# A graph layer and an attention layer on one core: own orders for the opening and the last group, and one pair of exponentials moved behind two copies

## The chip, the core and the metric

The kernel runs on one core of one Trainium2 chip. The metric is the device time of one execution in microseconds, taken as the median of several runs. A profiled execution adds a trace of every instruction on the engines: PE (TensorE matmuls; PEld is its weight loads), DVE (VectorE), ACT (ScalarE), POOL (GpSimd) and SP (SyncE, which here only issues DMAs).

## What is computed

There are 64 inputs of 256 nodes with 512 features, and one 256 x 256 adjacency matrix of ones and zeros. Layer 0 is a graph layer, layer 1 is attention with 8 heads of 64 over the same graph; each has a residual and a layernorm.

```python
def _L0_gnn_ref(x, adj, W, b):
    Wi, Wj = (W[:, :Din], W[:, Din:])
    mi = jnp.einsum('bkd,od->bko', x, Wi)
    mj = jnp.einsum('bkd,od->bko', x, Wj)
    deg = a.sum(axis=1)
    return deg[None, :, None] * (mi + b) + jnp.einsum('ij,bjo->bio', a, mj)
...
x = _layernorm(x + _L0_gnn_ref(x, adj, L0_gnn_W, L0_gnn_b), axis=-1)
# q, k, v = x @ W.T + b, split in heads; scores = q k / 8, -inf where adj == 0; softmax; @ v
x = _layernorm(x + _L1_gnn_ref(x, adj, Wq, bq, Wk, bk, Wv, bv, Wo, bo), axis=-1)
```

## The kernel before, in words

**Groups.** Two inputs are a group; there are 32 groups. The loop over g runs attention of group g and, in between, layer 0 of group g + 1, so that TensorE always has matmuls that do not wait for a softmax. Line numbers in this section are those of the kernel before; lines of the form L281 in the profile are those of the helper `matmul`, so groups of instructions are told apart by their tiles.

**Layer 0** of one input b (`l0_inputs`, L461, `l0_steps`, L483): x is split in a rounded part xhi and a rest xlo (`split_x`, L340, on ACT and POOL; POOL also adds the bias times degree, degb, to x). For each of four chunks of 128 features, four matmuls multiply xhi and xlo with `graph`, which holds diag(deg) and the transposed adjacency side by side, into a bank pa. ACT copies three quarters of it to xl (L475), and DVE makes the four sums xS from xl and pa (L478 to L481). Then seven steps, each four matmuls of 128 x 256, form the product with the weights by the seven-product scheme of Strassen and Winograd: the right-hand factors are the blocks of w0 and four combinations T1 to T4 of them, the left-hand ones xl and xS. DVE adds each result to xh (L497); steps 6 and 7 end in a layernorm (`norm`: statistics on DVE, the power -0.5 on POOL, shift and apply on ACT). `h_transpose` brings the result into hT, with features on partitions.

**Layer 1.** `qk_steps`, `v_steps` and `o_steps` use the same seven-product scheme for both inputs of a group at once: 28 matmuls of 128 x 256 each. Their factors (the weights' blocks and T1 to T4, made once by `make_factors` and kept in DRAM) are streamed in by `bring`, eight ahead. Attention goes in four slots, of two pairs of heads each: `scores` (L709), then on DVE the mask is added (L717), ACT takes the exponential (L721), POOL sums the two halves to pk (L724); `values` (L742) multiplies by v into pav, `divide` (L781) makes the denominators den, their reciprocal rden, spreads them with eight small DMAs and lets POOL multiply. The last slot of a group divides at once on DVE (L771, L772). `fold_value_bias` (L402) puts the value bias through wo into the output bias once.

**What sets the order.** The kernel is written in a tile framework which puts instructions on each engine's queue, and adds waits. Instructions under `in_order`, all matmuls among them, keep the program's order; the others the framework may move. Each engine works through its own queue in order. Banks of PSUM come from three pools: two double banks for scores (`score_banks`), one for pav, and three for everything else (`bank`), so that a product which takes a bank waits until the last reader of the bank's former tile is done.

**Around the change.** In the opening (L288 to L362) the DMAs are issued as: adjacency, x of input 0, the bias b_bc, four quarters of the layer 0 weights, x of input 1. DVE builds aT from the transposed adjacency, from that the tile `exact`, degb, and then `graph` as a rounded copy of exact; T1 to T4 of w0, a check that the rounding lost nothing (`inexact`), and maskT follow. Layer 0 of input 0 runs chunk by chunk, xhi and xlo in turn. Then come make_factors of wq, the fold, and the rest of group 0's layer 0, with the other make_factors between (L832 to L856). In slot u of a group the list `work[u]` of layer 0 items is run after the first of the slot's two exponentials; in the third slot the first item is `l0_inputs` of the group's second input, second half. The last group has no next layer 0: its slots stand alone, and then `o_steps` and `finish_steps` run as in every group.

Of the kernel before, what the change touches and what calls it, by code (L numbers as in the profile page):

```python
# [225 lines left out]
def unshifted_path(ctx, tc, flag, x, adj, wiT, wjT, b0, wqT, bq, wkT, bk, wvT, bv, woT, bo, out):  # L226
# [71 lines left out]
    nc.sync.dma_start(out=b_bc, in_=b0.to_broadcast([P, D]))  # L298
    w0 = const.tile([P, 7, NC, H], F32, name="w0")

    for n, w, j in ((B11, wiT, 0), (T3, wiT, 1), (B22, wjT, 1), (B21, wjT, 0)):
        nc.sync.dma_start(out=w0[:, n], in_=w.rearrange("(c p) o -> p c o", p=P)[:, :, j * H:(j + 1) * H])
    load_x(1)
# [21 lines left out]
    transposed_graph(nc, a, aT, ident, ps_m, "mm")  # L325
    deg = small.tile([P, NT], F32, tag="deg", name="deg")
    nc.vector.tensor_reduce(deg, a, AX.X, ALU.add)
    exact = p1.tile([P, NT, 3 * P], F32, tag="oS", name="exact")
    inexact = const.tile([P, 1], F32, name="inexact")
    for t in range(NT):  # L330
        nc.vector.tensor_copy(exact[:, t, (1 - t) * P:(3 - t) * P], aT[:, t, :])
        nc.vector.tensor_scalar(exact[:, t, 2 * t * P:(2 * t + 1) * P], ident, deg[:, t:t + 1], None, ALU.mult)
    for t in range(NT):
        nc.vector.tensor_scalar(degb[:, t, :], b_bc, deg[:, t:t + 1], None, ALU.mult)

    nc.vector.tensor_copy(graph, exact)
# [3 lines left out]
    def split_x(b):  # L340

        if b < B:
            xhi[b] = p1.tile([P, NT, D], F32R, tag="xhi", name="xhi")
            in_order(nc.scalar.copy(xhi[b], xh[b]))
            xlo[b] = p1.tile([P, NT, D], F32R, tag="xlo", name="xlo")
            in_order(nc.gpsimd.tensor_tensor(xlo[b], xh[b], xhi[b].bitcast(F32), ALU.subtract))
            in_order(nc.gpsimd.tensor_tensor(xh[b], xh[b], degb, ALU.add))

    split_x(0)

    def combine_right(f):

        in_order(nc.vector.tensor_sub(f(T1), f(T3), f(B11)))
        nc.vector.tensor_sub(f(T2), f(B22), f(T1))
        nc.vector.tensor_sub(f(T4), f(B21), f(T2))
        nc.vector.tensor_sub(f(T3), f(B22), f(T3))

    combine_right(lambda n: w0[:, n])
    nc.vector.tensor_tensor(exact, exact, graph.bitcast(F32), ALU.not_equal)
    nc.vector.tensor_reduce(inexact, exact.rearrange("p t n -> p (t n)"), AX.X, ALU.max)  # L360

    nc.vector.tensor_scalar(maskT, aT, 0.0, MASK, ALU.is_equal, ALU.mult)  # L362


    def load_bias(b, name):
        t = const.tile([P, NC], F32, tag=name, name=name)
        nc.sync.dma_start(out=t, in_=b)
        d = const.tile([P, 2], F32, tag=name + "d", name=name + "d")
        nc.vector.tensor_sub(d, t[:, 2:4], t[:, 0:2])
        return t, d  # L370

    bq_sb, bqd = load_bias(bq, "bq")
    bk_sb, bkd = load_bias(bk, "bk")
    bv_t = small.tile([P, NC], F32, tag="bvt", name="bv_t")
# [27 lines left out]
    def fold_value_bias(raw):  # L402

        pb = bank("pb")
        spread = p3.tile([P, NC, P], F32, tag="pk", name="spread")
        nc.vector.tensor_copy(spread, bv_t.unsqueeze(2).to_broadcast([P, NC, P]))
        for c in range(NC):
            h, kc = divmod(c, 2)
            nc.tensor.matmul(pb, spread[:, c], raw[:, h, kc].rearrange("p j o -> p (j o)"),
                             start=(c == 0), stop=(c == NC - 1))  # L410
        nc.vector.tensor_add(bo_bc, pb, bo_bc)
# [48 lines left out]

    def l0_inputs(b, half, borrow=False):  # L461


        if half == 0:
            xl[b] = p2.tile([P, NC, 3, P], F32, tag="xl", name="xl")
            a11, a12, a22 = (xl[b][:, :, m, :] for m in range(3))
            xS[b] = left_blocks(a11, a12, None, a22, p2.tile([P, 4, NC, P], F32, tag="xS", name="xS"))
        for c in (2 * half, 2 * half + 1):
            cs = slice(c * P, (c + 1) * P)
            pa = score_banks("pa")[:, 0, :] if borrow else bank("pa")  # L470
            parts = [(t, part) for t in range(NT) for part in (xhi[b], xlo[b])]
            for n, (t, part) in enumerate(parts):
                matmul(pa[:, t * P:(t + 3) * P], part[:, t, cs], graph[:, t, :],
                                 start=(n == 0), stop=(n == len(parts) - 1), skip_group_check=True)
            nc.scalar.copy(xl[b][:, c].rearrange("p m n -> p (m n)"), pa[:, :3 * P])  # L475
            _, a12, a22, a21 = (pa[:, m * P:(m + 1) * P] for m in range(4))
            f = xS[b]
            nc.vector.tensor_add(f["S1"][:, c], a21, f["A22"][:, c])  # L478
            nc.vector.tensor_sub(f["S3"][:, c], f["A11"][:, c], a21)
            nc.vector.tensor_sub(f["S2"][:, c], a22, f["S3"][:, c])  # L480
            nc.vector.tensor_sub(f["S4"][:, c], a12, f["S2"][:, c])  # L481
# [227 lines left out]
    def scores(g, u):  # L709


        made = []

        def exponentials(w, ps):
            i, pr = divmod(w, NC)
# [9 lines left out]
            made.append((pe, pk))  # L725

        later = []
        for w in (2 * u, 2 * u + 1):
            i, pr = divmod(w, NC)
            n0 = i * N  # L730
            ps = score_banks("ps").rearrange("p j (t q) -> p j t q", t=NT)
            for kc in range(NT):
                for j in range(2):
                    rows = slice(j * DH, (j + 1) * DH)
                    matmul(ps[:, j, kc, :], kT[g][rows, pr, n0 + kc * P:n0 + (kc + 1) * P],
                           qT[g][rows, pr, n0:n0 + N], start=True, stop=True)
            later.append(lambda w=w, ps=ps: exponentials(w, ps))
        return made, later

    products = []  # L740

    def values(g, u, made):  # L742
        i, half = divmod(u, NC // 2)
        n0 = i * N
        if u == 0:
            aoT[g] = p1.tile([P, NC, NB * N], F32, tag="aoT", name="aoT")
            oS[g] = pair_blocks(aoT[g], "oS")
        pav = ps_v.tile([P, 2, N], F32, tag="av", name="pav")
        for pp, (pe, _) in enumerate(made):
            for kc in range(NT):  # L750
                for j in range(2):
                    h0 = (2 * (2 * half + pp) + j) * DH
                    matmul(pav[j * DH:(j + 1) * DH, pp, :], vv[g][:, i, kc, h0:h0 + DH], pe[:, j, kc, :],
                           start=(kc == 0), stop=(kc == NT - 1))
# [3 lines left out]
        dst = aoT[g][:, 2 * half:2 * half + 2, n0:n0 + N]  # L758
        if u < SLOTS - 1:
            nc.scalar.copy(dst, pav)  # L760
            divide(dst, [pk for _, pk in made])
            return

        den = bank("den").rearrange("p (r q) -> p r q", r=2)
        for pp, (_, pk) in enumerate(made):
# [3 lines left out]
        for pp in range(2):  # L769
            rden = p2.tile([P, N], F32, tag="rden", name="rden")  # L770
            in_order(nc.vector.reciprocal(rden, den[:, pp, :]))  # L771
            in_order(nc.vector.tensor_mul(dst[:, pp, :], pav[:, pp, :], rden))  # L772
            inverses.append(rden)
        return inverses

    def end_values(g, inverses):
        combine_left(oS[g], in_order)
# [50 lines left out]
    for g in range(-1, NG):  # L828
        for name in (["wo"] if g >= 0 else []) + (["wq", "wk", "wv"] if g + 1 < NG else []):
            queue.extend((name, n) for n in (RIGHT_O if name == "wo" else RIGHT))  # L830

    load_x(2)  # L832
    raw_o, raw_q, raw_k, raw_v = (load_raw(w, t) for w, t in ((woT, "aoT"), (wqT, "kT"), (wkT, "v"), (wvT, "qT")))
    head = layer0(0)
    run(head[0])
    run(head[1])
    make_factors(wqT, "wq", raw_q)
    fold_value_bias(raw_o)
    run(head[2])
    make_factors(wkT, "wk", raw_k)  # L840
    run(head[3])
    make_factors(wvT, "wv", raw_v)
    run(head[4][:2])
    make_factors(woT, "wo", raw_o)
    for _ in range(AHEAD):
        bring()
    run(head[4][2:])
    q = qk_steps(0, qT, "qT", bq_sb, bqd)
    run(q[:1] + head[5] + head[6] + q[1:])
    run(with_output_bias(0, qk_steps(0, kT, "kT", bk_sb, bkd)))  # L850
# [5 lines left out]
    waiting, later = scores(0, 0)  # L856
    run(later + v[5:])
    for g in range(NG):
        more = g + 1 < NG
        load_x(NB * (g + 2))  # L860
        load_x(NB * (g + 2) + 1)
        work = layer0(g + 1) if more else [[] for _ in range(SLOTS + 3)]
        run(work[0])
        for u in range(1, SLOTS):
            values(g, u - 1, waiting)
            waiting, later = scores(g, u)
            run(later[:1] + work[u][:1] + later[1:] + work[u][1:])
        inverses = values(g, SLOTS - 1, waiting)
# [3 lines left out]
        end_values(g, inverses)  # L872
        run(rest[2:] + o[2:5] + work[SLOTS + 1] + o[5:6] + work[SLOTS + 2] + o[6:])
        end = finish_steps(g)
        if more:
            q = qk_steps(g + 1, qT, "qT", bq_sb, bqd)
            k = with_output_bias(g + 1, qk_steps(g + 1, kT, "kT", bk_sb, bkd))
            v = v_steps(g + 1)
            run(q[:5] + end[:1] + q[5:6] + end[1:2] + q[6:7] + end[2:3] + k[:1] + end[3:4] + k[1:] + end[4:] + v[:1])
            split_x(NB * (g + 2))  # L880
            run(v[1:5])
            waiting, later = scores(g + 1, 0)
            run(later + v[5:])
        else:
            run(end)
# [51 lines left out]
```

## Time and profile before

| what | us |
|---|---|
| median of 3 runs | 3264.04 (3263.74 to 3264.42) |
| the profiled execution, its own time | 3264.57 |
| its span in the trace | 3262.8 |
| mean granted TensorE clock | 0.997 of full speed |
| TensorE busy with matmuls | 3197.6 (98% of the span) |
| DVE, POOL, ACT busy | 1894.1, 1507.8, 1109.6 |
| DMA | 341.69 MB, mean 105 GB/s |

The profile's page gives busy time by engine, then the span in 40 slices of 81.6 us with a digit for the busy tenths of each. A line of a timeline gives start, duration, engine, line, operation, what it writes and reads (buffer numbers left out), and in brackets how long the engine was idle before it and what ended that. A line of the waits view gives who waited for whom, the sum, how many times and the longest. A stage line gives length, busy time of PE, PEld, DVE, ACT and POOL with the number of instructions, the granted clock, and what the DMA engines did. One matmul of the program in full float32 shows as two in the trace, 0.216 us apart for 256 columns at the full clock; the 384-column matmuls of the graph stage are in a rounded format and 0.18 us apart.

### The profile page before, as it was taken

The page shows a single profiled execution, that of the slowest core. Times are in us where ns is not written, and L with a number is a line of the kernel's source. Part 1 is how long each engine was busy: PE and PEld are TensorE (multiplying, and loading weights), DVE is VectorE, ACT ScalarE, POOL GpSimd, SP SyncE. Part 2 cuts the span into 40 slices and gives each one's busy share as a digit, 9 for nine tenths or more (in the row PEclk, how much of TensorE's full clock was granted, in tenths as well). Part 3 has the DMA queues.
Part 4 walks back from the last instruction along what each step waited for, and adds up shares of the span by engine and source line. Part 5 has one row for each costly group of instructions (what it writes and reads, how often), then busy time and mean ns, then how long its engine had stood idle before and what let it go on. Part 6 is the DMA issues. An engine that isn't in the chain of part 4 may idle for free. (4 is left out here: it accounts for less than half of the span.)

```text
span 3262.8 us, 48286 instructions
## 1 busy us (share of the span) xinstructions
PE 3197.6 (98%) x17422; PEld 2620.6 (80%) x17422; DVE 1894.1 (58%) x3852; ACT 1109.6 (34%) x2145; POOL 1507.8 (46%) x1193
## 2 busy tenths in 40 slices
PE   7999999999999999999999999999999999999997
PEld 6788887788887888878888778888788887888875
DVE  5655556555565555665555655556555566555564
ACT  2333333333333333333333334333333333333332
POOL 2454344544445444445434454444544444544443
PEclk9999999999999999999999999999999999999998
DMA  7234432344323344223333234432234432344322
GB/s 239 66 107 123 120 102 67 100 118 122 114 69 90 114 120 122 86 75 107 120 120 107 66 97 119 121 116 72 87 110 122 121 90 74 104 119 122 97 66 80
DMA packets 258000, 341.69 MB, mean 105 GB/s; under 512 B 29920, under 2 KB 155104, under 8 KB 257760
## 3 DMA queue, kind: packets, MB, share of 16 engines
q1 hardware_dynamic: 257760, 338.55, 34.8%
q8 instruction: 143, 2.34, 0.3%
q14 instruction: 97, 0.79, 0.1%
HBM read 275.52 MB, written 37.75 MB: 96 GB/s over the span
## 5 line engine op out<-in xcount | busy, mean ns | idle before, releaser
L439 POOL TENSOR_TENSOR rstd<-ve,mhalf 128x1 f32<-128x1 f32 x256 | 140.4, 549 | 822.3 <-DVE below L437 821.7
L281 PE MATMUL po<-w,xS 128*128 128x256 f32 x2048 | 474.3, 382 | 3.8
L281 PE MATMUL st<-hS,factor 128*128 128x256 f32 x2048 | 452.5, 379 | 0.0
L724 POOL TENSOR_TENSOR pk<-pe 128x512 f32<-128x512 f32 x256 | 323.2, 1273 | 269.3 <-ACT pe L721 269.3
L281 PEld LDWEIGHTS po<-w,xS 128*128 128x128 f32 x2048 | 383.9, 190 | 76.6 <-DVE xh L497 16.2
L281 PEld LDWEIGHTS st<-hS,factor 128*128 128x128 f32 x2048 | 389.1, 190 | 52.9
L281 PE MATMUL po<-w,xl 128*128 128x256 f32 x1536 | 366.7, 385 | 23.8 <-ACT xl L475 13.8
L721 ACT ACTIVATE pe<-pe 128x1024 f32<-128x1024 f32 x256 | 271.1, 1059 | 342.6 <-DVE pe L717 342.6
L281 PEld LDWEIGHTS po<-w,xl 128*128 128x128 f32 x1536 | 280.0, 190 | 91.2 <-ACT xl L475 26.2
L281 PE MATMUL st<-hT,factor 128*128 128x256 f32 x1536 | 343.9, 380 | 0.7 <-ACT hT L545 0.7
L603 DVE TENSOR_TENSOR u<-st,u 128x512 f32<-128x512 f32 x96 | 66.4, 692 | 476.3 <-PE st L281 464.2
L717 DVE TENSOR_TENSOR pe<-ps,maskT 128x1024 f32<-128x1024 f32 x256 | 296.9, 1201 | 65.3 <-PE ps L281 65.3
L497 DVE TENSOR_TENSOR xh<-po,xh 128x256 f32<-128x256 f32 (+1 forms) x384 | 173.4, 459 | 267.9 <-POOL xh L505 176.8
L281 PEld LDWEIGHTS st<-hT,factor 128*128 128x128 f32 x1536 | 292.9, 191 | 41.0 <-ACT hT L545 0.9
L281 PE MATMUL pav<-pe,v_sb 128*64 128x256 f32 x2048 | 251.8, 388 | 6.2 <-ACT pe L721 6.1
L281 PE MATMUL ps<-qT,kT 64*128 64x256 f32 x2048 | 256.3, 390 | 0.0
L281 PEld LDWEIGHTS ps<-qT,kT 64*128 64x128 f32 x2048 | 187.7, 187 | 67.7 <-issue 50.5
L281 PE MATMUL st<-factor,oS 128*128 128x256 f32 x1024 | 238.3, 381 | 2.2 <-issue 2.2
L281 PE MATMUL st<-factor,hS 128*128 128x256 f32 x1024 | 234.8, 382 | 0.0
L792 DVE RECIPROCAL rden<-den 128x256 f32<-128x256 f32 x96 | 168.8, 1758 | 97.1 <-PE den L281 93.4
L444 ACT ACTIVATE shift<-below,rstd 128x1 f32<-128x1 f32 x256 | 75.3, 294 | 427.0 <-POOL rstd L439 407.8
L281 PEld LDWEIGHTS st<-factor,hS 128*128 128x128 f32 x1024 | 191.9, 190 | 35.4 <-issue 10.6
(110 smaller groups left out, 5031.4 us busy)
## 6 DMA issues: line engine op xcount, KB each, us to landing
xh<-in_x_dram SPq DMA_DIRECT2D x64, 512.0 KB, 4.1
factor<-wq SPq DMA_DIRECT2D x128, 256.0 KB, 2.7
factor<-wk SPq DMA_DIRECT2D x128, 256.0 KB, 2.6
factor<-wv SPq DMA_DIRECT2D x128, 256.0 KB, 4.2
factor<-wo SPq DMA_DIRECT2D x128, 256.0 KB, 2.7
out_dram<-xh SPq DMA_DIRECT2D x64, 512.0 KB, 3.8
factor<-in_wqT_dram SPq DMA_DIRECT2D x96, 256.0 KB, 2.7
factor<-in_wkT_dram SPq DMA_DIRECT2D x96, 256.0 KB, 2.7
```

What stands on the lines that cost most here:

```text
L281: in_order(nc.tensor.matmul(*args, **kw))
L439: nc.gpsimd.tensor_tensor(rstd, ve, mhalf, ALU.pow)
L444: order(nc.scalar.activation(shift, below, AF.Identity, scale=rstd))
L497: nc.vector.tensor_add(dst, src, dst)
L603: nc.vector.tensor_add(new("u2"), bank["y"], k["u1"])
L717: nc.vector.tensor_add(pe.rearrange("p j t q -> p j (t q)"), ps.rearrange("p j t q -> p j (t q)"), maskT.rearrange("p t q -> p (t q)").uns ...
L721: in_order(nc.scalar.activation(flat, flat, AF.Exp, scale=QSCALE, accum_out=etot[:, NB * g + i, pr:pr + 1]))
L724: nc.gpsimd.tensor_tensor(pk, pe[:, :, 0, :], pe[:, :, 1, :], ALU.add)
L792: nc.vector.reciprocal(rden, den)
```

## The change

Three parts.

**The opening.** b_bc is loaded after the first quarter of w0. `graph` is written directly: two diagonals by DVE, then two copies out of the transposes' banks, with ACT copying the same banks to aT. degb, the bias differences and the check of `inexact` become functions that are called later. Input 0 is multiplied with all its xhi first, then all xlo (`first_inputs`), two of its banks borrowed from the scores' pool; step 3 of layer 0 comes ahead of step 2. The raw weights are loaded in the order wq, wk, wv, wo instead of wo, wq, wk, wv. make_factors and the fold go to other places: wq between the steps of input 0, wk before the steps of input 1, the fold after the first query product, wv and wo inside the query and key products, whose steps 2 and 3 change places for the query.

```diff
-    transposed_graph(nc, a, aT, ident, ps_m, "mm")
...
+    for t in range(NT):
+        nc.vector.tensor_scalar(graph[:, t, diagonal(t)], ident, deg[:, t:t + 1], None, ALU.mult)
+    for t in range(NT):
+        pt = bank("pt_a")[:, :N]
+        for i in range(NT):
+            transpose(pt[:, i * P:(i + 1) * P], a[:, i, t * P:(t + 1) * P], ident)
+
+        nc.vector.tensor_copy(graph[:, t, edges(t)], pt)
+        nc.scalar.copy(aT[:, t, :], pt)
...
+    def first_inputs(b):
+
+        input_tiles(b)
+        pas = [score_banks("pa")[:, 0, :] if c < 2 else bank("pa") for c in range(NC)]
+        for k, part in enumerate((xhi[b], xlo[b])):
+            for c in range(NC):
+                for t in range(NT):
+                    graph_product(b, c, pas[c], k * NT + t, t, part)
+                if k == 1:
+                    take_input(b, c, pas[c])
...
+    first_inputs(0)
+    in_order(nc.vector.tensor_sub(w0s[T3], w0s[B22], w0s[T3]))
+    p, q = l0_steps(0), l0_steps(1)
+    run([p[0], p[2], p[1]])
+    split_x(1)
+    run(p[3:5])
+    bias_steps()
     make_factors(wqT, "wq", raw_q)
-    fold_value_bias(raw_o)
-    run(head[2])
+    run(p[5:])
+    l0_inputs(1, 0, True)
+    l0_inputs(1, 1)
     make_factors(wkT, "wk", raw_k)
...
     q = qk_steps(0, qT, "qT", bq_sb, bqd)
-    run(q[:1] + head[5] + head[6] + q[1:])
-    run(with_output_bias(0, qk_steps(0, kT, "kT", bk_sb, bkd)))
+    run(q[:1])
+    fold_value_bias(raw_o)
+    h_transpose(1, 1, True)
+    h_transpose(1, 0, True)
+    run([q[2], q[1], *q[3:5]])
+    make_factors(wvT, "wv", raw_v)
+    run(q[5:])
+    k = with_output_bias(0, qk_steps(0, kT, "kT", bk_sb, bkd))
+    run(k[:4])
+    make_factors(woT, "wo", raw_o)
+    run(k[4:])
```

**The third slot.** `scores` and `values` now work on one pair of heads, and the loop calls them in twos in the same order as before. The one difference in groups 0 to 30: in the third slot both exponentials (mask, exponential, sum) stand after the first item of `work`, that is after the graph products of the second half and the copies of them; before, the first exponential stood ahead of it.

```diff
+            later = [scores(g, w), scores(g, w + 1)]
+            part = work[w // 2]
+            n = 0 if w == NB * NC - 2 else 1
+            run(later[:n] + part[:1] + later[n:] + part[1:])
```

**The last group** has code of its own. It goes pair by pair, with the scores two pairs ahead, and its output projection is plain: 16 matmuls of 128 x 512 with wo, which is loaded whole (1 MB) into the place of hT, instead of 28 of 128 x 256 and the sums. The first quarter of the projection stands ahead of the last pair's values, and each quarter is followed by its own addition, layernorm and store of 256 KB.

```diff
+    for w in range(last + 1):
+        values(g, w)
+        multiply()
+        if w == last - 1:
+            project(0, 0, (0, 1, 2, 3))
+            finish(0, 0)
+        elif w % 2 and w < last:
+            divide_two(g, w)
+        if w + 2 <= last:
+            scores(g, w + 2)()
+    inverses = divide_at_once(g, last)
+    project(0, 1, (0, 1, 2, 3))
+    finish(0, 1)
+    project(1, 0, (0, 1))
+    project(1, 1, (0, 1))
+    end_values(inverses)
+    for t in range(NT):
+        project(1, t, (2, 3))
+        finish(1, t)
```

## The prediction

> **What bounds the kernel now.** I read the page's busy shares first, then its slices, then busy time by stage, then TensorE's waits, then the timeline of one group.
>
> ```profile
> PE 3197.6 (98%) x17422; PEld 2620.6 (80%) x17422; DVE 1894.1 (58%) x3852; ACT 1109.6 (34%) x2145; POOL 1507.8 (46%) x1193
> ...
> PE   7999999999999999999999999999999999999997
> ```
>
> TensorE is the bound, and only the first and the last of the 40 slices (81.6 us each) are not full. The stages, cut at the first graph product (13.14), the first key product (73.68), the first value product (102.89), the last group's first scores (3201.68) and its first output product (3233.56):
>
> ```profile
> 0.00:13.14 13.14, 1.09 (x4) 0.75 (x5) 6.09 (x13) 2.33 (x2) 5.92 (x11) 1.00 0.78 257
> 13.14:73.68 60.54, 51.97 (x225) 43.45 (x225) 39.44 (x93) 13.88 (x29) 11.22 (x9) 0.97 0.71 245
> 73.68:102.89 29.21, 29.21 (x145) 25.32 (x143) 10.40 (x20) 8.94 (x17) 14.93 (x9) 1.00 0.52 143
> 102.89:3201.68 3098.79, 3074.97 (x16818) 2523.76 (x16817) 1804.45 (x3678) 1068.23 (x2068) 1451.01 (x1142) 1.00 0.35 102
> 3201.68:3233.56 31.88, 25.67 (x177) 15.33 (x176) 16.82 (x15) 11.46 (x20) 15.96 (x15) 0.89 0.14 39
> 3233.56:3262.80 29.24, 14.66 (x60) 11.95 (x58) 16.88 (x35) 4.79 (x9) 8.80 (x9) 0.83 0.11 39
> ```
>
> Length first, then TensorE's busy time, then the other engines; the third number from the end is the granted clock. TensorE idles 12 us before 13.14, 8.6 us up to 73.68, 24 us in the whole loop, 21 us after 3201.68. There is nothing else to win but work itself. The loop's 24 us are two waits per group:
>
> ```profile
> PE po L281 <- ACT xl L475: 13.8, 31, 0.8
> PE po L281 <- DVE xS L481: 10.0, 33, 2.6
> PE pa L281 <- DVE graph L336: 7.9, 1, 7.9
> PE pav L281 <- ACT pe L721: 6.1, 3, 2.2
> ```
>
> 31 waits of 0.445 us for the graph stage's copy xl, and (10.0 - 3.7 in the opening) / 31 = 0.20 us for xS. The third slot of one group:
>
> ```profile
> 1932.13 0.56 ACT L760 COPY aoT<-pav 128x512 f32<-128x512 f32 x1
> 1935.62 1.06 ACT L721 ACTIVATE pe<-pe 128x1024 f32<-128x1024 f32 x1 [2.92 <-DVE pe L717]
> 1936.58 0.19 ACT L721 ACTIVATION_READ_ACCUMULATOR pe<-pe 128x1 f32 x1
> 1936.67 0.84 ACT L475 COPY xl<-pa 128x384 f32<-128x384 f32 x2
> ...
> 1935.72 1.03 PE L281 MATMUL po<-w,xl 128*128 128x256 f32 x4
> 1937.18 1.13 PE L281 MATMUL po<-w,xl 128*128 128x256 f32 x4 [0.43 <-ACT xl L475]
> 1938.52 1.97 PE L281 MATMUL po<-w,xl 128*128 128x256 f32 x8 [0.20 <-DVE xS L481]
> ```
>
> ACT's copies stand behind the first exponential, though their graph product was complete at 1935.2.
>
> **The change: the loop.** Set side by side, the two programs differ in groups 0 to 30 in one thing: ACT's two xl copies now stand ahead of the first exponential. The order on PE, DVE, POOL and SP and what each waits for are the same. The first copy can start at 1935.2 (the fourth pa matmul starts at 1934.85 and takes 0.34), the second at 1935.95, both done by 1936.4; the matmul that waited till 1937.18 was due at 1936.60. That wait goes. What is late next is the x bank's successor: step 2 takes a bank whose last reader is an xS subtraction on DVE, and DVE adds two masks first (L717, 1934.42, 2.29 us), till 1936.7. Then xS begins at 1936.7 instead of 1937.16, and step 2 starts 1.36 us behind that as now (1938.52 - 1937.16): 1938.06. **0.45 us a group, times 31: 14 us.** Bounds: nothing, if DVE holds step 2 where it is; and the whole start-to-start excess of both places, (1937.18 - 1936.60) + (1938.52 - 1938.04) = 1.06 us, 33 us. I take 14, since the DVE rows set it. What is queued behind: both exponentials end at about 1938.6 as now (the second waited for DVE until 1937.4 anyway, they follow each other in 1.1 us); the first pk sum on POOL comes 0.8 us later, the second 0.1, and the denominators that need them stand at 1944.79. So the exponentials' delay is hidden under the 4 us of step products and transposes.
>
> **The opening.** Now DVE waits for b_bc until 8.16 (degb), then makes exact, aT, maskT and graph, and the first pa starts at 13.14. After: a 3.61 to 4.04, deg to 4.76, two diagonals (0.47 for both) to 5.25, two copies out of the transposes' banks straight to graph (0.37 each, the aT row) to 6.0; ACT copies aT behind them (0.37 each) to 6.5, then xhi (1.04): pa at 7.6, **5.5 us sooner**. Here the row is 6.0 for the graph, and ACT's aT copies wait for DVE's in the built program.
>
> [...]
>
> From there by hand: 16 pa matmuls (twelve at 0.32, as in the rows after 13.14, then 0.18) to 12.3; step 1 to 14.0. The last quarter of w0 lands at 14.0 as before, T4 needs it (1.21) to 15.25, then 16 xS operations start 0.20 apart; the 14th frees step 2's bank at 18.2. So the wait for xS stays (1.9 us, was 2.6). Step 2 and four more, 1.73 each, to 26.9; the second graph's pa (2.9, now without its 1.7 wait) to 29.75; its step 1 waits 1.15 for the last xl copy, which stands on ACT behind two layernorm operations; seven steps and two transposes to 44.1. Query product 1 to 45.85. The value-bias fold (8 x 0.43) now stands where TensorE waited for the second graph's layernorm (2.5 + 0.7 us, and a half-rate stretch to 64.7); it waits 0.75 for its spread behind that layernorm's DVE chain, ends at 50.05; transposes 0.85, six products 10.4: 61.35. Then a new wait: DVE does the last qT addition (0.88 for two) and only then the u3 one, and the key's first product takes the bank that they free: 1.15. **Key products start at 62.5 instead of 73.68: 11 us.** Bounds: 5.5, if all later waits come back as they are; 5.5 + 8.6 + 1.7 (the half-rate stretch) = 15.8.
>
> **The last group.** Now each slot waits through scores, two mask additions, two exponentials (7.4 to 7.9 us a slot), then come output products 1, two reciprocals (1.76 each), the S sums, 7 products, four layernorms in a row, two 512 KB stores. After, pair by pair: a slot is a chain of mask (1.15), exponential (1.06), pk (1.27) and denominators (0.6), with a value product (0.9), a score product (1.0) and DVE's reciprocal (1.76) and other mask between: followed row by row, denominators start at 3210.1, 3216.2, 3222.3 and 3229.1, the last at 3232.6 now. The plain projection is 16 matmuls of 128x512, 0.86 each by the pb row (3.60 for eight halves), 13.8 us where 28 of 0.43 took 12.1 at full clock: 1.7 us more. But four stand ahead of the last pair, two thirds of the rest needs no last reciprocal, and no S sums come between: the last twelve run 3229.95 to 3240.4. Then one addition 0.69, stats 0.68 + 0.4, rstd 0.55, shift 0.30, apply 0.81 with their hand-overs: 3244.1; a 256 KB store 2.8 (a factor of that size lands 2.7 after issue) and the 1.5 that follow the last landing now: 3248.5. **14 us.** Bounds: 4, if all of the twelve run at half rate (10.3 more); 18, if the slots shrink to two exponentials and a denominator each.
>
> A row that bears on this: after waits of 2.2 us the value products at 3229.24 ran in 3.53 us instead of 1.95, and the granted clock of the last two stages is 0.89 and 0.83. The new order's longest wait is 1.3 us. [...]
>
> By the row one such stretch costs 3.53 - 1.95 = 1.6 us, and the sum with one is 12.4; I keep 14, since 1.3 us is nearer to the 0.5 us waits that leave the clock alone in the loop's third slot than to 2.2.
>
> On SP: in the opening x of graph 2, then wv and wo stand ahead of the factor stores, which land behind the last of these (28.8) and by 33, before the query products at 44; in the last group the 1 MB load of wo is issued at a value product near 3196 and wanted at 3224.8, and the 24 spread transfers (0.63 apart, last landing 6.3 us after the reciprocal) are the same, the third in time for 3233. Nothing else: the bias differences, check_graph (4.3 us of DVE) and the later factor stores stand under step products, whose DVE has room; without that cover each 1 us of them moves the second graph's steps by as much.
>
> **Sum** against the profiled execution (span 3262.8, time 3264.57, 0.5 above the median 3264.04): 3264.6 - 11 - 14 - 14 = 3225.6.
>
> **Rivals.** *The loop gives nothing:* DVE's masks and reciprocals keep xS where it is. For it: DVE, not ACT, releases the second wait. Against it: xS began within 0.1 us of the copies' end. 3264.6 - 25 = 3239.6. *The loop gives all:* if step 2 does not wait for that bank, 25 + 33 = 58: 3207. Against it: the bank order is the same. *The ends lose:* the opening keeps only its 5.5 and the projection is at half rate, 5.5 + 14 + 4: 3241. *Slower:* the delayed exponentials hold POOL's pk sums so long that the third slot's denominators wait; the place is den at 1944.79, pk ends at 1939.9 now, so it decides from a delay of 4.9 us on, and to end above 3271 each group must lose 1.0 us more than that with the ends' 25 kept. Only a cause that the rows do not show (ACT blocked by its copies for 5 us) does this.
>
> **Chances.** As forecast (3214 to 3235) 0.70; loop nothing 0.10; loop all 0.07; ends lose 0.06; no difference that counts 0.03; slower 0.04. 0.2% (6.5 us) is about what a measurement can tell from no change. Faster is 0.93. The range 3212 to 3241 takes in the first, second and fourth, 0.86, less what lies outside the terms' bounds.
>
> **What would show it.** Loop: the wait for xl gone from 31 to none, that for xS grown from 0.20 to about 0.4 each, group period 0.45 shorter. Opening: first pa near 7.6, fold between the query products, key products near 62. End: last denominators to span's end near 19 us, now 30. I am wrong if the xS wait swallows the gain, if new waits for pe or den appear in the loop, or if the clock falls below 0.8 in the projection.

## The result, and the profile after

The changed kernel takes 3232.61 us (median of five runs, 3228.02 to 3232.79) against 3264.04: ratio 0.990, interval 0.9885 to 0.9914. It is 31 us faster; the forecast was 39 (3225.6, range 3212 to 3241). The profiled execution took 3232.61 us with a span of 3230.8.

The page, engine shares and TensorE's slices:

```profile
PE 3189.2 (99%) x17398; PEld 2617.4 (81%) x17398; DVE 1892.0 (59%) x3847; ACT 1113.0 (34%) x2146; POOL 1506.9 (47%) x1191
...
PE   8999999999999999999999999999999999999998
```

Busy time by stage, cut at the first graph product, the first key product, the first value product, the last group's first scores and the first output product behind the last denominators:

```profile
0.00:7.33 7.33, 1.08 (x4) 0.71 (x4) 2.26 (x6) 2.93 (x4) 1.13 (x9) 1.00 0.63 202
7.33:66.88 59.55, 52.21 (x225) 43.00 (x225) 43.45 (x96) 14.08 (x29) 18.35 (x10) 0.97 0.75 260
66.88:100.65 33.77, 31.27 (x145) 26.48 (x145) 18.83 (x25) 8.95 (x17) 16.54 (x9) 0.95 0.54 160
100.65:3182.57 3081.92, 3066.66 (x16818) 2527.32 (x16817) 1798.78 (x3678) 1071.40 (x2068) 1450.13 (x1142) 1.00 0.35 103
3182.57:3211.68 29.11, 27.21 (x185) 15.17 (x185) 18.70 (x20) 11.22 (x20) 15.89 (x14) 1.00 0.14 41
3211.68:3230.80 19.12, 10.77 (x28) 4.77 (x26) 9.95 (x26) 4.43 (x8) 4.84 (x7) 0.89 0.17 60
```

The first stage lost 5.8 us (forecast 5.5), but the second only 1.0, and the third grew by 4.6. To add up without overlap I cut at the starts of the groups' value products: group 0's begin at 100.65 (102.89 before), group 31's at 3188.15 (3207.26), the span ends at 3230.82 (3262.79).

| part | before | after | gain | forecast |
|---|---|---|---|---|
| opening, to group 0 | 102.89 | 100.65 | 2.2 | 11 |
| loop, 31 groups | 3104.37 | 3087.50 | 16.9 | 14 |
| last group to the end | 55.53 | 42.67 | 12.9 | 14 |

TensorE's waits after:

```profile
PE po L281 <- DVE xS L492: 15.9, 32, 4.5
...
PE st L281 <- DVE u L636: 2.5, 1, 2.5
...
PE po L281 <- ACT xl L486: 0.4, 1, 0.4
```

The wait for xl is gone from the loop (the one left is in the opening); that for xS is (15.9 - 4.5) / 31 = 0.37 us a group. Two long waits stand in the opening: 4.5 us for xS, and 2.5 us for u in the key products, where the forecast had 1.9 and none. In the third slot DVE's masks, ACT's copies and step 2 stand like this (start, duration, then in brackets the idle time before):

```profile
1922.39 2.29 DVE L756 TENSOR_TENSOR pe<-ps,maskT 128x1024 f32<-128x1024 f32 x2
...
1923.18 0.48 ACT L486 COPY xl<-pa 128x384 f32<-128x384 f32 x1 [2.53 <-PE pa L281]
...
1924.59 0.28 DVE L489 TENSOR_TENSOR xS<-pa,xl 128x128 f32<-128x128 f32 x1
...
1925.94 1.32 PE L281 MATMUL po<-w,xl 128*128 128x256 f32 x5 [0.36 <-DVE xS L492]
```

The copies start when their graph products are done (the second, at 1923.89, too), and the first exponential follows at 1924.26; xS starts when the second mask ends, and step 2 is 1.35 us behind xS, as the forecast said.

**Where the opening went.** DVE and POOL, 10 to 20 us:

```profile
10.33 1.21 DVE L879 TENSOR_TENSOR w<-w 128x1024 f32<-128x1024 f32 x1
10.56 3.23 POOL L373 TENSOR_TENSOR xh<-xh,degb 128x1024 f32<-128x1024 f32 x1 [0.82 <-DVE degb L360]
11.47 2.60 DVE L356 TENSOR_SCALAR maskT<-aT 128x512 f32<-128x512 f32 x1
13.99 3.96 DVE L879 TENSOR_TENSOR w<-w 128x1024 f32<-128x1024 f32 x2
14.44 2.44 POOL L538 TENSOR_TENSOR xh<-xh,u 128x768 f32<-128x768 f32 x1 [0.65 <-ACT u L535]
16.84 3.32 POOL L370 TENSOR_TENSOR xlo<-xh,xhi 128x1024 fp32r<-128x1024 f32 x1
```

All but the first are too long: T2 and T4 take 3.96 where T1 took 1.21, maskT 2.60 where before it took 0.41, POOL's three take 3.23, 2.44 and 3.32 where before they took 2.45, 1.82 and 2.34. Nobody is slow: by the ends of these rows each waits for the other to finish. POOL's sum starts when T1 ends (about 11.5) and ends at 13.79; maskT does its 0.4 behind that. T4, ready at 15.2, finds POOL at work till 16.88 and ends 1.1 later, at 17.96; POOL's xlo, started at 16.84, then runs from 17.96 to 20.16. T4 was to end at 15.25, so step 2 starts at 20.88 and not at 18.3.

### The profile page after: what moved, and what is told of

The parts are those of the page before. It is cut to its first block, busy times and chain, and to the rows that moved or that the text cites. A ratio compares the mean times of both kernels' runs of the same rounds, so it can differ in the third digit from the quotient of the medians.

```text
span 3230.8 us, 48219 instructions
## 1 busy us (share of the span) xinstructions
PE 3189.2 (99%) x17398; PEld 2617.4 (81%) x17398; DVE 1892.0 (59%) x3847; ACT 1113.0 (34%) x2146; POOL 1506.9 (47%) x1191
## 3 DMA queue, kind: packets, MB, share of 16 engines
q8 instruction: 143, 2.34, 0.3%
## 5 line engine op out<-in xcount | busy, mean ns | idle before, releaser
L281 PE MATMUL po<-w,xl 128*128 128x256 f32 x1536 | 360.1, 384 | 16.8 <-DVE xS L492 15.9
L281 PE MATMUL st<-factor,oS 128*128 128x256 f32 x992 | 229.4, 379 | 0.0
```

The source lines that it names most:

```text
L281: in_order(nc.tensor.matmul(*args, **kw))
```

## The experiments

**1. The loop's order alone**, on the kernel before:

```diff
-            run(later[:1] + work[u][:1] + later[1:] + work[u][1:])
+            n = 0 if u == SLOTS - 1 else 1
+            run(later[:n] + work[u][:1] + later[n:] + work[u][1:])
```

> The kernel before with the third slot's order alone changed. From the two traces the group period fell from 100.22 to 99.68 us, 31 x 0.54 = 16.9 us. If that is the third slot and nothing else, this kernel takes 3264.0 - 16.9 = 3247 us and shows the period 99.68; the forecast's own term (0.45 a group, 14 us) would give 3250. Rival: the period fell because of something that the new opening sets up (the phase of the factor loads), and the order alone gives nothing: 3264.

Measured: 3246.32 us, ratio 0.9948 (0.9934 to 0.9962), 17.7 below before; the period, the median distance of two groups' first value products, is 99.68. These products run from 103.93 (group 0) to 3191.46 (group 31), so the 31 groups take 3087.5 us, as in the change. The loop's gain is that order, and nothing in the opening is needed for it. The rest of the 17.7 lies outside the loop: the opening is 1.0 us longer than before, and from group 31 on it takes 53.1 us instead of 55.5, with the old code. In the kernel before, TensorE fell to half rate three times in this stretch ahead of its last output product (granted clock 0.50 in 3215.42 to 3218.83, 3229.07 to 3232.48 and 3242.73 to 3246.13). The mean granted clock of the whole execution is 0.997 in both, so that fewer such stretches make the difference is not shown.

**2. The old opening** in the changed kernel, twice. The first try held the spread and the fold of the value bias in program order, which the kernel before did not: the eight matmuls of the fold (L409) are the exception to the rule that all matmuls keep the program's order.

> The changed kernel with the opening of before (loop and last group as changed). The first value product of group 0 started at 102.90 us before and at 100.65 after, so the new opening is worth 2.3 us in the profiled execution: 3232.6 + 2.3 = 3234.9 us expected here. Rival: the opening is worth the 11 us that the forecast gave it and something behind the first value product took them back: 3243.6 us.

Measured: 3241.15 us, neither number. My edit was not the old opening: the fold waited 3.4 us for its spread and group 0 began at 109.55. The second try leaves both to the scheduler:

```diff
-        in_order(nc.vector.tensor_copy(spread, bv_t.unsqueeze(2).to_broadcast([P, NC, P])))
+        nc.vector.tensor_copy(spread, bv_t.unsqueeze(2).to_broadcast([P, NC, P]))
...
-            matmul(pb, spread[:, c], raw[:, h, kc].rearrange("p j o -> p (j o)"),
+            nc.tensor.matmul(pb, spread[:, c], raw[:, h, kc].rearrange("p j o -> p (j o)"),
```

> Again the changed kernel with the opening of before; now the spread of the value bias and the fold may be moved by the scheduler as before (in the run old_open they were held in order, the fold waited 3.5 us and group 0 began at 109.55 instead of 102.90). Group 0's first value product should be back near 102.9 and the time at 3264.0 - 16.9 - 12.9 = 3234.2, or 3232.6 + 2.3 = 3234.9: 3234 to 3236. Rival, the opening worth 11 us: 3243.6.

Measured: 3234.48 us, group 0 at 103.18. With the loop's order and the last group alone, 29.2 us of the change's gain are there. The new opening adds 2 to 4 us to that, not 11 (1.9 to the median of the change above, 4.1 to that of experiment 7; all four runs lie above all nine runs of the change). What the parts of the new last group, its order by pairs and its plain projection, are worth one by one was not run.

**3. What delays T4: maskT, or POOL?**

```diff
-        nc.vector.tensor_scalar(maskT, aT, 0.0, MASK, ALU.is_equal, ALU.mult)
+        in_order(nc.vector.tensor_scalar(maskT, aT, 0.0, MASK, ALU.is_equal, ALU.mult))
```

> The changed kernel with the making of maskT kept behind the second input's steps, so that DVE runs T1, T2, T4 in a row. In the trace after, maskT took 2.60 us (11.47 to 14.07) between T1 and T2 and step 2 started at 20.88 instead of the forecast 18.3. Theory A (DVE and POOL exclude each other while both work on SBUF, and maskT was long only because POOL's sum of xh and degb ran from 11.45 to 13.79): T2 takes maskT's place and waits as long, T4 still ends near 17.8, step 2 starts at 20.6 to 20.9 and the time stays at 3232.4. Theory B (maskT is simply 2.6 us of DVE work in the way): step 2 at 18.3, no half-rate stretch behind it, 3232.6 - 2.5 - 1.7 = 3228.4.

Measured: 3228.37 us (3226.61 to 3230.41), which is theory B's number, but not by B's way. The unedited change itself ran in 3228.0 to 3232.8 us, so here the trace has to tell. T2 and T4 still took 4.29 us for two: T2 was held from 11.85 till POOL's sum ended at 13.80, as A said. Then POOL's next sum came only at 15.00, when T4 was already running, and this time POOL waited (2.81 us for its 1.82). Step 2 started at 19.06, between the two theories' times, and a half-rate stretch came all the same: its eight matmuls took 3.56 us, against 1.97 in the next run. That each of the two engines waits for the other I had right; who starts first I misjudged. The other edit takes POOL's sum away instead:

```diff
             if b == 0:
-                degree_bias()
+                for t in range(NT):
+                    r = xh[b][:, t, :]
+                    in_order(nc.vector.scalar_tensor_tensor(r, b_bc, deg[:, t:t + 1], r, ALU.mult, ALU.add))
+                return
...
     first_inputs(0)
+    degree_bias()
```

> The changed kernel with POOL's sum of xh and degb for input 0 replaced by two DVE operations (bias times degree plus xh) ahead of T1; degb itself is made later; maskT may stand where the scheduler puts it. Theory A (exclusion): with no POOL sum beside them T1 runs to 12.1, T2 and T4 take 1.21 each and T4 ends near 14.9, the last quarter of w0 landing at 13.24; step 2 starts at 17.3 to 17.9 with a wait near 1.3 us and no half-rate stretch behind it: 3232.6 - 3.3 - 1.7 = 3227.6, less what later waits take back. maskT takes 0.41 instead of 2.60. Theory B (the DVE queue is just too long): DVE gets 1.4 us more work ahead of T1, step 2 starts at 21 or later and the time is 3233 or more.

Measured: 3224.51 us (3224.36 to 3225.77), below every run of the change. DVE's two operations take 1.41 us where degb took 1.67, T1 starts 0.9 us later than in the change, and T4 is done 2.9 us sooner:

```profile
11.20 1.22 DVE L882 TENSOR_TENSOR w<-w 128x1024 f32<-128x1024 f32 x1
...
12.53 1.22 DVE L882 TENSOR_TENSOR w<-w 128x1024 f32<-128x1024 f32 x1
13.87 1.22 DVE L882 TENSOR_TENSOR w<-w 128x1024 f32<-128x1024 f32 x1
...
17.41 1.97 PE L281 MATMUL po<-w,xl 128*128 128x256 f32 x8 [0.88 <-DVE xS L495]
```

T1, T2 and T4 take 1.22 each, maskT 0.43 (at 6.47, ahead of all of them), and no half-rate stretch follows: step 2's eight matmuls take 1.97. Theory B is out: with maskT out of the way but POOL's sum in place, in the run above, T2 was held all the same. The time is 3.1 us below A's number. The key's fourth product also waited only 1.2 us here, 1.3 less than in the change, and by DVE's rows no half-rate stretch followed that either, which A did not count in: from u (L639, 71.40) to the next sum (L645, 74.17) it took 2.77 us, where the change took 3.42 with the clock at 0.50, and 2.78 in its second profile (experiment 7) with the clock at 1.00.

**4. The key's fourth product.** After the change the factors of wo are made on DVE beside POOL's sums of the output bias:

```profile
69.65 5.56 POOL L584 TENSOR_TENSOR xh<-xh,bo_bc 128x1024 f32<-128x1024 f32 x2
70.34 2.65 DVE L411 TENSOR_TENSOR t<-raw,t 128x512 f32<-128x512 f32 x1
...
72.92 2.83 DVE L411 TENSOR_TENSOR t<-raw 128x512 f32<-128x512 f32 x1
...
77.54 0.69 DVE L636 TENSOR_TENSOR u<-st,u 128x512 f32<-128x512 f32 x1 [1.18 <-DMA wo<-t]
78.28 0.92 PE L281 MATMUL st<-hS,factor 128*128 128x256 f32 x3 [2.50 <-DVE u L636]
```

The edit moves the sums behind the key's steps:

```diff
-    k = with_output_bias(0, qk_steps(0, kT, "kT", bk_sb, bkd))
-    run(k[:4])
+    k = qk_steps(0, kT, "kT", bk_sb, bkd)
+    run(k[:3])
     make_factors(woT, "wo", raw_o)
-    run(k[4:])
+    run(k[3:])
+    add_output_bias(0)
+    add_output_bias(1)
```

> The changed kernel with POOL's two sums of xh and the output bias behind the key's seven steps, so that they no longer run beside the factors of wo on DVE. Theory A (exclusion of DVE and POOL): the four factor subtractions take 0.69 each from about 69.7 on (after it was 1.32, 2.65, 2.83, 0.68), the wait of the fourth key product for u (2.5 us in the profiled run) goes, and no half-rate stretch follows: 3232.6 - 2.7 - 1.7 = 3228.2 us. Rival B (the wait is for the store of a factor, whose buffer u takes): the wait shrinks only to the 1.2 us that were put down to the store, the time is 3231 or, with the half-rate stretch gone as well, 3229.5, and DVE's rows are short all the same.

Measured: 3230.53 us, inside the change's own spread, so again the trace decides, and for rival B, although the wait is 2.1 us and not the 1.2 that B gave. The second and third factor, 2.65 and 2.83 before the edit, are short now, and the wait is still there:

```profile
70.42 0.69 DVE L411 TENSOR_TENSOR t<-raw,t 128x512 f32<-128x512 f32 x1
...
74.67 0.69 DVE L411 TENSOR_TENSOR t<-raw,t 128x512 f32<-128x512 f32 x1 [2.95 <-DMA wo<-t]
77.22 0.69 DVE L636 TENSOR_TENSOR u<-st,u 128x512 f32<-128x512 f32 x1 [1.86 <-DMA wo<-t]
77.96 1.35 PE L281 MATMUL st<-hS,factor 128*128 128x256 f32 x5 [2.10 <-DVE u L636]
```

The last factor and u wait for buffers that earlier factors leave only when their store has landed. Behind one wait stood another of nearly its length. So the next kernel adds other buffers, of tiles that are unused at that time:

```diff
-        t1, t2, t3, t4 = (p4.tile([P, 2, H], F32, tag="u", name="t") for _ in range(4))
+        t1, t2, t3, t4 = (pool.tile([P, 2, H], F32, tag=tag, name="t")
+                          for pool, tag in pools or [(p4, "u")] * 4)
...
+    make_factors(woT, "wo", raw_o, [(p2, "spread")] * 2 + [(p3, "pk")] * 2)
```

> The kernel of the run bias_late (3230.5 us) with the four factors of wo made in buffers that no later sum of the key waits for. In bias_late DVE's rows were short but u, for the fourth key product, still waited 1.86 us for the store of a factor to land (at 77.1). If the wait had two layers, POOL's sums and behind them the store, this kernel shows no wait of the fourth key product and no half-rate stretch there: 3230.5 - 2.3 = 3228.2 us, and group 0's first value product at 96.3 instead of 98.6. Rival (a third layer, such as the factor loads that SP issues behind the stores): a wait of over 1 us stays and the time is 3229.5 or more.

Measured: 3228.9 us; the wait is gone from the list. Group 0 began at 95.62, 3.0 us sooner than in bias_late. Of these, 1.4 come from step 2 (19.60 instead of 20.97), because T4 happened to start ahead of POOL in this run; so the buffers gave 1.6, not 2.3.

**5. What holds step 2 in the loop**, on top of dve_bias: in the third slot the first mask, then xS, then the second mask.

```diff
+            if w == NB * NC - 2:
+                later[0].mask(in_order)
+                xs_order[0] = in_order
+                run(part[:1])
+                xs_order[0] = anywhere
+                later[1].mask(in_order)
+                run(later + part[1:])
```

> The kernel of the run dve_bias (3224.5 us) with one more edit, in the loop: in the third slot DVE does the first mask, then the eight xS operations, then the second mask. Theory A (the wait that took the xl wait's place, 0.36 to 0.52 us a group, is there because both masks, 2.3 us, stand ahead of xS on DVE): the period falls from 99.68 to between 99.16 and 99.32 and the time to 3224.5 - 11 to - 16 = 3208.5 to 3213.5. Rival B (the second exponential, its pk sum and ACT's copy of u now come about 1 us later, and value products, denominators or step 3 wait for them): the period stays or grows, 3224 to 3240.

Measured: 3210.03 us (3209.33 to 3210.18); period 99.09. The first mask, xS and the second mask now stand in this order, and TensorE runs steps 1 and 2 (16 matmuls) without a wait:

```profile
1905.86 1.16 DVE L764 TENSOR_TENSOR pe<-ps,maskT 128x1024 f32<-128x1024 f32 x1
...
1907.16 3.62 PE L281 MATMUL po<-w,xl 128*128 128x256 f32 x16
1907.17 0.29 DVE L493 TENSOR_TENSOR xS<-pa,xl 128x128 f32<-128x128 f32 x1
...
1909.26 1.21 DVE L764 TENSOR_TENSOR pe<-ps,maskT 128x1024 f32<-128x1024 f32 x1
```

TensorE's waits:

```profile
PE den L281 <- POOL pk L777: 2.0, 3, 0.9
...
PE po L281 <- DVE xS L496: 0.5, 1, 0.5
```

Theory A holds: the 31 waits for xS are gone, and the rival's waits for pk appear in three places only, 2.0 us in all. The 31 groups take 3072.8 us instead of 3087.4, 14.6 less, which is the whole gain of 14.5.

**6. All edits together.**

> Opening, key phase and loop edits together (dve_bias, bias_late, xs_first). If they add up: xs_first less the 1.4 us that the fourth key product still waited in the run dve_bias. Rival: the POOL sums moved behind the key's steps delay the split of the next input and the first graph products wait: no gain over xs_first or a loss of 1 to 2 us.

Measured: 3210.65 us, no gain, which is the rival's number but not its cause: no graph product waited for the split. The key's fourth product still waited 1.7 us. The store of a factor landed 0.13 us before u started, and the profile puts the wait down to an operation of ACT's that ended after that, so the trace alone doesn't say which held it. With the other buffers as well:

> dve_bias, bias_late, xs_first and the other buffers for wo's factors together. xs_first took 3210.0 us and its fourth key product waited 1.5 us; without that wait 3208.5. Rival: the two POOL sums in their later place delay the next input's split or the third slot of the first groups, as in best1 (3210.65): 3210 to 3211.

Measured: 3208.41 us (3207.28 to 3208.57), ratio to before 0.9829 (0.9816 to 0.9843). All its runs are faster than those of the kernel without the other buffers (3209.35 to 3213.23). It is 55 us below before and 24 below the change.

**7. The change again**, for its spread.

> The changed kernel once more, unedited, beside the two others: its five runs lay between 3228.0 and 3232.8 us. If the spread comes from whether the waits of step 2 (4.5 us) and of the fourth key product (2.5 us) are followed by a stretch at half rate (1.7 us each), the runs of this one spread over about the same 4 us and the profiled run shows the time to go with the number of such stretches: two at 3232.7, one at 3231, none at 3229.3. Rival: the stretches are there in every run and the spread is of the length of the waits themselves, which move with the landing of the loads.

Measured: 3230.34 us (3228.0 to 3231.74). The profiled run, 3231.74, has a half-rate stretch behind step 2's wait (granted clock 0.50 in 21.70 to 26.40) and none behind the key's (1.00 from 50 to 100). By the mean clock of 0.92 over 7.5 to 50.0 it is about 6.8 us long, twice the length of each of the change's two (3.41); the step 2 wait was 3.9 and the key's 2.7. So both move. POOL's xh sum started at 15.34 and T4 could start at 15.50: POOL won, T2 and T4 took 3.97. In wo_both POOL came at 15.59 and T4 at 15.42: DVE won, 2.47 for both. A difference of 0.2 us decides about 1.5. That this race and the stretches make the whole spread isn't shown, since only one run of each is profiled. What is shown is where it arises: in all eight profiles that have the change's loop and last group as they are, the time from group 0's first value product to the end is the same within 0.8 us.

## Why the prediction came out as it did

**The loop, right; size 14, measured 16.9 (17.7 alone).** The xl wait went, the x bank's successor was next, at 0.37 instead of "0.4". The period fell by 0.54, not 0.45: xS starts 0.90 us behind step 1's start where I had put it at 0.98. The masks stand where they stood (1.30 us ahead of step 1, 2.29 long); xS starts 0.09 before their row ends, and I had let it start at the end. Both rivals on the loop are out, and no new wait for pe or den came. The condition of the rival that gives all, "if step 2 does not wait for that bank", is what xs_first made true by another edit, which frees the bank in time: 14.6 us more in the loop, 31.5 with the 16.9, where that rival had put 33.

**The last group, right; size 14, measured 12.9, or 10.4 against the old code as it ran in experiment 1.** Last denominators to the end took 19.4 us (forecast 19). The slots took 23.2 us from the first value product to the last denominators, my rows 21.8: value products waited twice, 0.8 and 1.0, for an exponential. TensorE kept its full clock up to the last output product (1.00 over 3182.57 to 3222.33), as I took it.

**The opening, wrong in size: 11, measured 2.2, below its bound of 5.5.** The start was as worked out: first graph product at 7.33 (7.6), step 1 at 11.99 (12.3). The step that failed is "T4 needs it (1.21) to 15.25". Alone it takes that, beside POOL it took 2.72, and maskT, which I had left with check_graph "under step products", stood ahead of T2. That cost 2.6 us, and the half-rate stretch behind the longer wait (0.50 over 21.45 to 24.86) 1.5: the second graph's products began at 31.08 instead of 26.9, the key's at 66.88 instead of 62.5. The second failure is that the wo factors, costed at nothing under the key products, made a wait of 2.5 us and another half-rate stretch (0.50 over 79.48 to 82.89): from the first key to the first value product it took 33.77 us instead of 29.21, 4.6 more, of which 2.5 are idle and 2.1 slower work. In sum 11.2 - 4.4 - 4.6 = 2.2, as measured. My lower bound failed for the same reason: it let old waits come back, and these are new ones.

The trace of before could have told. There POOL was idle from 11.8 to 20.3, while DVE made T1 to T4, but two DVE copies met a POOL operation, one on either side of that:

```profile
9.39 2.45 POOL L347 TENSOR_TENSOR xh<-xh,degb 128x1024 f32<-128x1024 f32 x1 [0.82 <-DVE degb L334]
...
10.23 1.96 DVE L331 COPY exact<-aT 128x256 f32<-128x256 f32 x2
...
22.04 2.35 POOL L346 TENSOR_TENSOR xlo<-xh,xhi 128x1024 fp32r<-128x1024 f32 x1
...
22.29 2.39 DVE L406 COPY spread<-bv_t 128x512 f32<-128x512 f32 x1
```

In the trace after, where POOL has no long operation beside them, a copy to exact takes 0.28 and the one to spread 0.41. 22.04 + 2.35 + 0.41 is 24.80, and the copy to spread ended at 24.68; for the first copy to exact the same sum gives 12.12, and it ended at 11.99. I took durations from quiet rows and moved the operations beside busy ones.

The sum was right to 7 us: the opening fell 9 short, the last group 1, and the loop gave 3 more. That the loop's surplus covered a third of the opening's miss was luck. The sign rested on the loop and the last group. Experiment 1 confirms the loop alone; the last group was not run alone, and experiments 1 and 2 confirm it by their difference, 11.8 us.

## What to carry to other kernels

Here several DVE rows whose operands all lie in SBUF waited for a POOL operation, and POOL's rows for them (maskT 2.60 us instead of 0.41, the sum of xh and degb 3.23 instead of 2.45). Where an edit brings two such rows together, add the one's duration to the other's, and ask which starts first; look in the old trace for rows of the same shape that take several times their usual time. When the wait on the critical path is taken away, price the next one at the same place before calling the place done: here the xl wait hid the xS wait and the POOL sums hid a store. And where an engine has two jobs of which only one frees a bank, put the other behind it: moving one mask was worth 14.5 us, more than the whole new last group.

## What the runs showed of the hardware

**DVE and POOL side by side.** maskT took 0.43 us in dve_bias and 2.60 in the change, T4 1.22 and 2.72, factors of wo 0.69 (bias_late) and 2.83. Each of the long ones ended where POOL's operation ended plus its own time, and POOL's rows were held the same way: in the change its sum of xh and degb took 3.23 and xlo 3.32, where before they took 2.45 and 2.34. The ends agree with these sums to 0.15 us. xS, which reads pa from PSUM, was not held: it took 0.27 to 0.29 from 17.88 on, under POOL's xlo (up to 20.16). Nor was every operation whose operands all lie in SBUF: in the change BATCH_NORM_STATS2 took 0.68 to 0.70 in all 256 cases, one of them at 3216.72, under POOL's additions of rtot (3215.62 to 3217.15). What sets the two kinds apart no run tested.

**The clock.** A line gives the window, its length, TensorE's busy time and, third from the end, the granted clock. The key's fourth product waited 2.50 us in the change's first profile. These are the 3.41 us that hold the wait, and the 3.41 us behind them:

```profile
76.07:79.48 3.41, 1.20 (x6) 1.07 (x7) 0.98 (x2) 0.59 (x2) 0.00 (x0) 1.00 0.97 299
79.48:82.89 3.41, 3.41 (x10) 2.65 (x9) 1.38 (x2) 0.00 (x0) 1.10 (x1) 0.50 0.56 183
```

and these the same wait, 2.7 us, in the second profile of the same kernel, and what followed it:

```profile
76.70:79.70 3.00, 0.35 (x2) 0.00 (x0) 1.62 (x3) 0.84 (x2) 0.00 (x0) 1.00 0.89 307
79.70:83.00 3.30, 3.29 (x15) 2.93 (x16) 1.23 (x2) 0.00 (x0) 0.43 (x1) 1.00 0.85 233
83.00:90.00 7.00, 7.00 (x34) 6.15 (x34) 1.03 (x3) 2.12 (x3) 3.92 (x3) 1.00 0.56 151
```

A wait of 2.5 us was followed by 3.41 us at half rate, one of 2.7 us at the same place was not, so the length of the wait alone does not tell. Step 2's wait was followed by 3.41 us at 0.50 in the first profile (wait 4.5, stretch 21.45 to 24.86) and by about 6.8 in the second (wait 3.9). The waits of 0.37 us a group left the clock at 1.00 from 100.65 to 3182.57. What decides between the waits of 2.5 and 2.7 us is not shown: no run shifted a wait on purpose to test this.
